# Eight gated blocks on one core: inverse square roots moved to VectorE, an MLP bias folded into a matmul, and three stages issued in written order

## The chip, the cores and the metric

The kernel runs on one core of a Trainium2 chip, in one launch. The metric is the device time of that launch in microseconds (us). A core has five engines that work side by side and meet only through semaphores: TensorE (PE; its weight loads are listed apart as PEld), VectorE (DVE), ScalarE (ACT), GpSimd (POOL) and SyncE (SP, which here only issues DMAs). Each engine takes its own instructions in the order in which they stand in its queue; an instruction whose semaphore is not there yet holds back all that stand behind it on that engine.

## The reference, cut to what matters

Four gated layers act on `x` of shape (16, 128, 128): 16 batches, 128 tokens, 128 features. Each layer adds a cross attention over a context of 77 rows and then a feed-forward block, each on a layer-normed `x` and scaled by the tanh of a gate:

```
x = x + tanh(g_xattn[i]) * Li_xattn(layernorm(x), ctx)
x = x + tanh(g_ffn[i])   * Li_ffn(layernorm(x))
```

The change touches three of the eight blocks. `L0_xattn` and `L2_xattn` are attentions with 16 heads of 8 features. `L0_ffn` is itself a stack of six transformer layers, and most of the time goes there:

```
for i in range(6):
    x = attn_layer(shift_tokens(x), ...) + x     # 16 heads of 64, q and k divided by their norms,
                                                 # rotary factors, window of 32, then Wo
    x = ffn_layer(shift_tokens(x), ...) + x      # layernorm, W1, a * gelu(gate), W2 + b2
```

`q` and `k` are divided by `max(norm, 1e-12)`; the second matmul of the MLP adds a bias `b2`.

## The kernel before

`X` lies in SBUF as four tiles of four batches each (groups `g` of 0 to 3, `GB` = 4). Everything is float32, apart from the attention mask. Blocks follow each other in the program: `l0_xattn`, `l0_ffn`, `l1_xattn` and so on. Within them a list scheduler of the Tile layer decides the order in which each engine's instructions stand: it takes what it thinks ready first, so that an engine's order is not that of the source.

**The heads of eight** (class `AttentionOf8`, called by `l0_xattn` and `l2_xattn`) go batch by batch in a software pipeline written in `run`: in round `n` the weights of batch n-2 are transposed (`turned`), the scores of batch n are made, masked and exponentiated (`scores`: PE, DVE L246 and L251, POOL L252, ACT L253), batch n-3 is mixed with its values (`mixed`), the weights of batch n-1 are divided by their sums (`normed`: DVE L257 and L258, POOL L259), and batch n-4 is projected and added to `X`. Scores have one PSUM buffer (tag `s`), all other PSUM tiles share four (tag `m`).

**The six layers** (`l0_ffn`) go by half units: a unit is one batch in one layer, and a half is 8 of its 16 heads. Step `k` of the loop takes five half units at different stages:

- half k ("a"): `l0_project` multiplies by Wqkv (PE L454), forms the rotary products out of PSUM (DVE L457, two of 128x1024), squares the same PSUM tile (ACT L462), sums the squares (DVE L463) and adds the rotary halves (POOL L466); `l0_values` makes the values (PE L471, ACT L473). After the second half of a unit, `l0_norms` turns the 32 sums of squares of each token into inverse roots: a maximum on POOL (L479), a first guess by an exponential of the bits (ACT L483), two Newton steps of four POOL instructions each (L485 to L488), and two POOL products that scale q and k (L492).
- half k-3 ("b"): `l0_turn` transposes q and k (PE, helper line L189) and copies them out; `l0_scores` makes masked scores (PE L505, L509), the row maximum (DVE L512), eight exponentials with their sums (ACT L516), and then the reciprocal (DVE L517) and the division (POOL L518).
- half k-5 ("c"): `l0_turn_p` transposes the weights (PE L189), `l0_mix` multiplies by the values (PE L532, copied by ACT L534).
- half k-7 ("d"): after the second half, `l0_add` multiplies by Wo (PE L540) and adds to `Y` (DVE L541).

A step with even `k` thus has `l0_add`; a step with odd `k` has `l0_norms`. At fixed steps, twice in each layer, two groups pass the MLP: `l0_mlp_norm` (token shift by a matmul, statistics on DVE L554 and L555, root on POOL L557 to L560, the bias b2 added to `Y` by POOL L561, normalised by ACT L563), two steps later `l0_mlp_turn` (transpose, gain and bias), and then `l0_mlp_out` for one group at a time (W1 on PE L576, gelu on ACT L578, product on DVE L579, W2 on PE L583, sum on DVE L584). PSUM is shared between two buffers of two banks for the big tiles (tag `s`: `ps_qk`, `ps_s`, `ps_h`) and four of one bank (tag `m`: all others).

Two engines that read the same PSUM tile are kept one after the other by the Tile layer, so the squares of L462 come after both products of L457.

Of the kernel before, what the change touches and what calls it, by code (L numbers as in the profile page):

```python
# [9 lines left out]
F32 = mybir.dt.float32  # L10
# [77 lines left out]
def tile_gated_layers(ctx: ExitStack, tc: tile.TileContext, io, out: bass.AP):  # L88
# [70 lines left out]

    def copy(i, out_, in_):  # L160

        if i % 2:
            nc.scalar.copy(out_, in_)  # L163
        else:
            nc.vector.tensor_copy(out_, in_)
# [7 lines left out]
    def layernorm(pool, out_, in_):  # L173

        st = pool.tile([128, GB, 6], F32, name="ln_st", tag="ln_st")
        mv = pool.tile([128, GB, 2], F32, name="ln_mv", tag="ln_mv")
        rs = pool.tile([128, GB], F32, name="ln_rs", tag="ln_rs")
        for j in range(GB):
            nc.vector.bn_stats(st[:, j, :], in_[:, j, :])
            nc.vector.bn_aggr(mv[:, j, :], st[:, j, :])  # L180
        rsqrt(pool, rs, mv[:, :, 1], GB, 1e-5)
        for j in range(GB):
            nc.vector.tensor_scalar(out_[:, j, :], in_[:, j, :], mv[:, j, 0:1], rs[:, j : j + 1], ALU.subtract, ALU.mult)

# [26 lines left out]
    class AttentionOf8:  # L211
# [28 lines left out]
        def scores(self, u, qT, kb):  # L240
            ps = self.psum.tile([128, 4, 512], F32, name="ps_s", tag="s")
            for c in range(4):
                at = slice(32 * c, 32 * c + 32)
                nc.tensor.matmul(ps[:, c, : 4 * S], lhsT=qT[at], rhs=kb[at], start=True, stop=True)
# [4 lines left out]
            )  # L249
            mx = self.pool.tile([128, 16], F32, name="mx", tag="mx")  # L250
# [10 lines left out]
        def turned(self, u):  # L261
            pT = u.pT = self.pool.tile([S, 16, 128], F32, name="pT", tag="pT")
            for c in range(4):
# [3 lines left out]
                nc.scalar.copy(pT[:, 4 * c : 4 * c + 4, :], pt[:S])  # L267

        def mixed(self, u, v):
            po = self.psum.tile([128, 4, 128], F32, name="ps_o", tag="m")  # L270
            for c in range(4):
                for t in range(4):
                    nc.tensor.matmul(po[32 * t : 32 * t + 32, c, :], lhsT=v[:, 4 * c + t, :], rhs=u.pT[:, 4 * c + t, :], start=True, stop=True)
            u.oT = self.pool.tile([128, 4, 128], F32, name="oT", tag="oT")
            nc.vector.tensor_copy(u.oT, po)

        def out(self, u):
# [3 lines left out]
            return pr  # L281

        def run(self, group, values, layer):

            class U:
                pass

            us = {}
            for n in range(-1, B + 4):
                if (n + 1) % GB == 0 and n + 1 < B:  # L290
                    ready = group((n + 1) // GB)
                    us.update({n + 1 + j: U() for j in range(GB)})
                    for j in range(GB):
                        us[n + 1 + j].qT, us[n + 1 + j].kb = ready[0][:, j, :], ready[1][:, :, j, :]
                if 0 <= n - 2 < B:
                    self.turned(us[n - 2])
                if 0 <= n < B:
                    self.scores(us[n], us[n].qT, us[n].kb)
                if 0 <= n - 3 < B:
                    self.mixed(us[n - 3], us[n - 3].v)  # L300
                if 0 <= n - 1 < B:
                    u = us[n - 1]
                    self.normed(u)
                    u.v = self.values(n - 1, values(n - 1))
                if 0 <= n - 4 < B:
                    pr = self.out(us[n - 4])
                    gated((n - 4) // GB, (n - 4) % GB, pr, tanh_x, layer)


    def l0_xattn():  # L310
        with tc.tile_pool(name="a0", bufs=2) as pool, tc.tile_pool(name="a0p", bufs=1, space=PSUM) as ps1, tc.tile_pool(
# [5 lines left out]
            def group(g):  # L317
# [5 lines left out]
                kb = attention.keys(kT)  # L323
                z = pool.tile([128, GB, 128], F32, name="z", tag="z")
                layernorm(pool, z, X[g])
                ps = transposed(psum, z)
                zT = pool.tile([128, GB, 128], F32, name="zT", tag="zT")
                nc.scalar.copy(zT, ps)
# [4 lines left out]
                return qT, kb  # L333
# [6 lines left out]
            attention.run(group, values, 0)  # L340


    def l0_ffn(weights):


        with tc.tile_pool(name="b0y", bufs=1) as ypool, tc.tile_pool(name="b0w", bufs=2) as wpool, tc.tile_pool(
# [12 lines left out]
            nc.vector.memset(seed, 0.5 * float(np.log(2.0)) * (127.0 - 0.043))  # L359
            W = {}  # L360
# [8 lines left out]
            for l in range(DEPTH):  # L369
                for part in range(2):  # L370
                    at = 2 * B * l + B * part + B + 7
                    pair = [_Mlp(l, 2 * part + i) for i in range(2)]
                    mlps.setdefault(at, []).extend((l0_mlp_norm, m) for m in pair)
                    mlps.setdefault(at + 2, []).extend((l0_mlp_turn, m) for m in pair)
                    mlps.setdefault(at + 3, []).append((l0_mlp_out, pair[0]))
                    mlps.setdefault(at + 5, []).append((l0_mlp_out, pair[1]))
# [9 lines left out]
            for k in range(2 * len(units) + B):  # L386
                a, ah = half_unit(k)
                b, bh = half_unit(k - 3)
                c, ch = half_unit(k - 5)
                d, dh = half_unit(k - 7)  # L390
                if a and ah == 0:
                    a.start(pool, W[a.l], xT[a.g][:, a.j, :])
                if b:
                    l0_turn(pool, psum, b, bh)
                if a:
                    l0_project(pool, psum, a, ah)
                if d and dh == 1:
                    l0_add(psum, d, Y[d.g][:, d.j, :])
                for part, m in mlps.get(k, ()):
                    part(pool, psum, W[m.l], Y[m.g], m)  # L400
                if c:
                    l0_turn_p(pool, psum, c, ch)
                if b:
                    l0_scores(pool, psum, b, bh, masks)
                if a:
                    l0_values(pool, psum, a, ah)
                if c:
                    l0_mix(pool, psum, c, ch)
                if a and ah == 1:
                    l0_norms(pool, a, seed)  # L410

                n, nh = half_unit(k + 2)
                if n and nh == 0 and n.j == 0:
                    shift(n)
# [3 lines left out]
    def l0_weights(wpool, l):  # L418
# [10 lines left out]
        w["b2"] = wpool.tile([128, 128], F32, name="w_b2", tag="w_b2")  # L429
        nc.sync.dma_start(out=w["b2"], in_=io["l0_b2"][l : l + 1].to_broadcast([128, 128]))  # L430
# [45 lines left out]
    def l0_norms(pool, u, seed):  # L476

        ss = u.ss.rearrange("p g a h -> p (g a h)")
        nc.gpsimd.tensor_scalar_max(ss, ss, 1e-24)  # L479
        y = pool.tile([128, 32], F32, name="nw_y", tag="nw_y")  # L480
        t = pool.tile([128, 32], F32, name="nw_t", tag="nw_t")

        nc.scalar.activation(y, ss.bitcast(I32), AF.Exp, bias=seed, scale=-0.5 * float(np.log(2.0)) / 2.0**23)  # L483
        for c in (1.0 + 1.67e-4, 1.0):
            nc.gpsimd.tensor_tensor(t, y, y, ALU.mult)  # L485
            nc.gpsimd.tensor_tensor(t, t, ss, ALU.mult)
            nc.gpsimd.tensor_scalar(t, t, -0.5 * c, 1.5 * c, ALU.mult, ALU.add)
            nc.gpsimd.tensor_tensor(y, y, t, ALU.mult)  # L488
        y = y.rearrange("p (g a) -> p g a", g=2)
        for g in range(2):  # L490
            r = u.r[g].rearrange("p a h d -> p (a h) d")
            nc.gpsimd.tensor_tensor(r, r, y[:, g].unsqueeze(2).to_broadcast([128, 16, 64]), ALU.mult)  # L492
# [7 lines left out]
    def l0_scores(pool, psum, u, g, masks):  # L500
# [16 lines left out]
        nc.vector.reciprocal(rs, rs)  # L517
        nc.gpsimd.tensor_tensor(p, p, rs.unsqueeze(2).to_broadcast([128, 8, 128]), ALU.mult)  # L518
        u.p.append(p)

# [22 lines left out]
    def l0_mlp_norm(pool, psum, w, Y, m):  # L543

        xs = m.xs = pool.tile([128, GB, 128], F32, name="xs", tag="xs")
# [536 lines left out]
```

## Time and profile before

| | |
|---|---|
| three timed runs | 3258.79, 3260.86 and 3262.26 us; median 3260.86 |
| the profiled execution's own time | 3258.67 us |
| its span in the profile | 3256.9 us, 50402 instructions |
| mean granted clock of TensorE | 0.915 of full speed |
| busy share of the span | PE 85%, PEld 58%, DVE 58%, ACT 54%, POOL 55% |
| `l0_xattn`, from the start | to 166 us |
| `l0_ffn` | 166 to 2205 us |
| `l2_xattn` | some 2555 to 2715 us |

The profile is one execution. Its views used here are: the table by stretch of time (busy time of each engine and the granted clock), the timeline (start, duration, engine, line, tiles; in brackets how long the engine had stood idle before and which instruction ended that), the list of waits, and the groups of instructions with the mean duration of one. A busy share is a mean over stages with different limits, so each stage has to be read by itself.

### The profile page before, as it was taken

Reading aid. Unit: us, or ns where it says so; the run is one execution under the profiler, and the core shown is the slowest. Engines: PE = TensorE matmul, PEld = TensorE weight load, DVE = VectorE, ACT = ScalarE, POOL = GpSimd, SP = SyncE. Lnnn points to the kernel's source line nnn. Section 1 sums busy time; section 2 is a strip of 40 time slices with the busy share of each in tenths; the row PEclk is TensorE's granted clock in tenths of the full one; section 3 lists DMA queues with packets and bytes.
Section 4 is the critical chain, followed back from the end, with each engine's and each line's share of the span. In section 5 each row is a group of like instructions: output and inputs, shape, how many; then the busy total and the mean of one; then the engine's idle time right before and its main releaser. Section 6 shows DMA issues by size and latency. Waiting matters only on the chain.

```text
span 3256.9 us, 50402 instructions
## 1 busy us (share of the span) xinstructions
PE 2756.5 (85%) x18912; PEld 1888.0 (58%) x18912; DVE 1876.6 (58%) x3163; ACT 1745.7 (54%) x5161; POOL 1778.9 (55%) x2030
## 2 busy tenths in 40 slices
PE   5779898989899898989898989898889678985656
PEld 4546565656566565656565656565655455653445
DVE  5566555555656564656565656545337765456553
ACT  3448676667667676758676767672222342222221
POOL 5568867686858585868776767751000451013222
PEclk8889999999999999999999999998779788997777
DMA  1020000000000000000000000002000000000003
GB/s 54 1 70 1 1 21 9 8 1 1 28 7 1 1 28 7 1 1 21 7 8 1 1 1 1 1 1 82 1 1 1 1 2 1 1 1 1 1 1 117
DMA packets 24304, 40.15 MB, mean 12 GB/s; under 512 B 1790, under 2 KB 18940, under 8 KB 22908
## 3 DMA queue, kind: packets, MB, share of 16 engines
q1 hardware_dynamic: 21036, 26.96, 2.5%
q0 software_dynamic: 2448, 9.07, 0.9%
q8 instruction: 149, 2.44, 0.3%
q10 hardware_dynamic: 576, 0.91, 0.1%
q14 instruction: 95, 0.78, 0.1%
HBM read 35.88 MB, written 1.05 MB: 11 GB/s over the span
## 4 chain that ended last, share of the span: by engine, by line
PE 46%; POOL 21%; ACT 15%; DVE 12%; issue 5%; DMA 1%; DVEq 0%; ACTq 0%; POOLq 0%
ACT p L516 7%; PE ps_t L189 7%; PE ps_qk L454 5%; POOL p L518 4%; POOL r L466 4%; PE ps_h L778 4%; POOL r L492 4%; PE ps_s L509 3%; PE ps_v L471 3%; DVE r L457 3%; PE ps_o L532 3%; PE ps_r L583 2%; PE ps_d L784 2%; PE ps_p L266 2%; PE ps_h L576 2%
## 5 line engine op out<-in xcount | busy, mean ns | idle before, releaser
L518 POOL TENSOR_TENSOR p<-p,rs 128x1024 f32<-128x1024 f32 x192 | 364.1, 1896 | 432.7 <-DVE rs L517 381.2
L516 ACT ACTIVATE p<-ps_s,mx 128x128 f32<-128x128 f32 x1536 | 539.6, 382 | 14.6 <-DVE mx L512 9.3
L457 DVE TENSOR_TENSOR r<-ps_qk,w_turn 128x1024 f32<-128x1024 f32 x384 | 454.2, 1215 | 140.2 <-PE ps_qk L454 74.8
L466 POOL TENSOR_TENSOR r<-r 128x512 f32<-128x512 f32 x384 | 480.7, 1271 | 9.5 <-DVE r L457 9.4
L454 PE MATMUL ps_qk<-w_qkv,xT 128*128 128x512 f32 x768 | 363.6, 596 | 5.3 <-ACT sq L462 3.3
L492 POOL TENSOR_TENSOR r<-r,nw_y 128x1024 f32<-128x1024 f32 x192 | 361.5, 1901 | 7.5
L516 ACT ACTIVATION_READ_ACCUMULATOR p<-ps_s,mx 128x1 f32 x1536 | 340.6, 222 | 0.0
L463 DVE TENSOR_REDUCE ss<-sq 128x16 f32<-128x1024 f32 x192 | 234.0, 1219 | 106.3 <-ACT sq L462 106.2
L189 PEld LDWEIGHTS ps_t<-const,p 128*128 128x128 f32 x1536 | 178.4, 143 | 168.8 <-ACT oT L534 110.3
L512 DVE TENSOR_REDUCE mx<-ps_s 128x8 f32<-128x1024 f32 x192 | 233.8, 1218 | 46.7 <-PE ps_s L509 46.7
L462 ACT ACTIVATE sq<-ps_qk 128x1024 f32<-128x1024 f32 x192 | 201.8, 1051 | 105.6 <-DVE r L457 103.2
L509 PEld LDWEIGHTS ps_s<-rT 64*128 64x128 f32 x3072 | 192.5, 193 | 104.1 <-ACT pT L163 49.0
L532 PEld LDWEIGHTS ps_o<-pT,v 128*64 128x64 f32 x3072 | 164.8, 137 | 122.4 <-issue 45.4
L509 PE MATMUL ps_s<-rT 64*128 64x128 f32 x3072 | 229.5, 290 | 5.8 <-ACT rT L163 5.8
L189 PE MATMUL ps_t<-const,r 128*128 128x128 f32 x1536 | 210.9, 281 | 17.2 <-POOL r L492 17.2
L471 PE MATMUL ps_v<-w_qkv,xT 128*128 128x512 f32 x384 | 224.6, 669 | 0.0
L505 PE MATMUL ps_s<-masks 128*128 128x512 bf16 x384 | 124.6, 392 | 116.8 <-ACT p L516 115.3
L473 ACT COPY v<-ps_v 128x512 f32<-128x512 f32 x192 | 114.3, 595 | 199.8 <-PE ps_v L471 199.8
L540 PEld LDWEIGHTS ps_r<-w_o,oT 128*128 128x128 f32 x1536 | 185.6, 192 | 59.5 <-issue 38.8
L189 PE MATMUL ps_t<-const,p 128*128 128x128 f32 x1536 | 212.3, 280 | 8.3 <-POOL nw_y L488 4.7
L532 PE MATMUL ps_o<-pT,v 128*64 128x128 f32 x3072 | 211.9, 279 | 1.8 <-ACT pT L163 1.2
L517 DVE RECIPROCAL rs<-rs 128x8 f32<-128x8 f32 x192 | 38.6, 201 | 300.5 <-ACT p L516 300.3
(265 smaller groups left out, 5275.9 us busy)
## 6 DMA issues: line engine op xcount, KB each, us to landing
w_qkv<-in_l_qkv SPq DMA_DIRECT2D x6, 1536.0 KB, 8.0
w_o<-in_l_o SPq DMA_DIRECT2D x6, 512.0 KB, 4.0
w<-in_l SPq DMA_DIRECT2D x6, 341.0 KB, 5.7
l_g<-in_l_g SPq DMA_DIRECT2D x1, 1152.0 KB
l_u<-in_l_u SPq DMA_DIRECT2D x1, 1152.0 KB, 11.1
l_d<-in_l_d SPq DMA_DIRECT2D x1, 1152.0 KB, 13.8
X<-in_x SPq DMA_DIRECT2D x4, 256.0 KB
l_kv<-in_l_kv SPq DMA_DIRECT2D x2, 512.0 KB, 14.4
```

What stands on the lines that cost most here:

```text
L189: nc.tensor.transpose(ps[:, j, :], in_[:, j, :], ident)
L454: nc.tensor.matmul(ps[:, a, :], lhsT=u.xT, rhs=u.w["qkv"][:, a * 1024 + g * 512 : a * 1024 + g * 512 + 512], start=True, stop=True)
L457: nc.vector.tensor_tensor(r12[:, :, a], ps[:, a].rearrange("p (h d) -> p h d", d=64).unsqueeze(1).to_broadcast([128, 2, 8, 64]), u.w["turn ...
L463: nc.vector.tensor_reduce(u.ss[:, g], sq.rearrange("p a (h d) -> p a h d", d=64), AX.X, ALU.add)
L466: nc.gpsimd.tensor_tensor(r[:, :, :, lo : lo + 32], r12[:, 0, :, :, lo : lo + 32], r12[:, 1, :, :, hi : hi + 32], ALU.add)
L471: nc.tensor.matmul(pv, lhsT=u.xT, rhs=u.w["qkv"][:, 2048 + g * 512 : 2048 + g * 512 + 512], start=True, stop=True)
L492: nc.gpsimd.tensor_tensor(r, r, y[:, g].unsqueeze(2).to_broadcast([128, 16, 64]), ALU.mult)
L509: nc.tensor.matmul(ps[:, o_, c, :], lhsT=u.rT[at, 0, c, :], rhs=u.rT[at, 1, c, :], start=False, stop=True, skip_group_check=True)
L512: nc.vector.tensor_reduce(mx, ps, AX.X, ALU.max, negate=True)
L516: nc.scalar.activation(p[:, h, :], ps[:, h, :], AF.Exp, bias=mx[:, h : h + 1], accum_out=rs[:, h : h + 1])
L518: nc.gpsimd.tensor_tensor(p, p, rs.unsqueeze(2).to_broadcast([128, 8, 128]), ALU.mult)
L532: nc.tensor.matmul(po[64 * o_ : 64 * o_ + 64, c, :], lhsT=u.v[g][:, 2 * c + o_, :], rhs=u.pT[:, 4 * o_ + c, :], start=True, stop=True)
```

## The change

1. **Order.** The loops of `AttentionOf8.run` and of `l0_ffn` are run inside `in_order`, which takes them out of the list scheduler's hands: PE, DVE, ACT and POOL issue these stages' instructions in the order in which the source emits them.
2. **Roots on VectorE.** In `l0_norms` the maximum before the root goes, the two Newton steps become six DVE instructions on a guess that now lies in PSUM (tag `m`), and a seventh DVE instruction bounds the result. The two scaling products stay on POOL.
3. **Division a step later.** The reciprocal and the division of `l0_scores` become `l0_divide`, called one step later, after `l0_project`.
4. **The bias b2.** It becomes an 86th row of the last part of W2; the matching row of the hidden tile is set to one once, and the POOL addition L561 goes. One DMA row of 128 floats replaces a DMA that spread the bias over 128 rows.
5. **The MLP in finer parts.** Statistics of both groups together at the end of step `at` (after `l0_norms`), normalisation at the end of step `at`+1, transposes at `at`+3, outputs at `at`+4 and `at`+6.
6. **Heads of eight in finer parts.** The layernorm is split into statistics (three rounds ahead), application on ACT (two rounds ahead, with the keys) and transposes (one round ahead); the transposes of the weights go in two halves around the scores; the copy of `oT` goes from DVE to ACT, and in `l2_xattn` the key bias too.

The diff, cut to its core:

```diff
+    def in_order(f, *args):
+        ET = mybir.EngineType
+        with tc.manual_schedule(engines={ET.PE, ET.DVE, ET.Activation, ET.Pool}):
+            f(*args)
...
+    def ln_stats(pool, in_):
...
+        for j in range(GB):
+            nc.vector.bn_stats(st[:, j, :], in_[:, j, :])
+        for j in range(GB):
+            nc.vector.bn_aggr(mv[:, j, :], st[:, j, :])
+        nc.gpsimd.tensor_scalar_add(rs[:, 0], mv[:, :, 1], 1e-5)
+        nc.gpsimd.tensor_tensor(rs[:, 0], rs[:, 0], minus_half[:, :GB], ALU.pow)
...
+    def ln_apply(out_, in_, rs):
+        for j in range(GB):
+            nc.scalar.activation(out_[:, j, :], in_[:, j, :], AF.Identity, bias=rs[:, 1, j : j + 1], scale=rs[:, 0, j : j + 1])
...
+            for n in range(-4, B + 4):
+                for k in (3, 2, 1):
...
+                if unit(n - 2):
+                    self.turned(us[n - 2], 0)
+                if unit(n):
+                    self.scores(us[n])
+                if unit(n - 2):
+                    self.turned(us[n - 2], 1)
+                if unit(n):
+                    self.exps(us[n])
+                if unit(n - 3):
+                    self.mixed(us[n - 3])
+                if unit(n - 1):
+                    self.normed(us[n - 1])
+                    us[n - 1].v = self.values(n - 1, values(n - 1))
+                if unit(n - 4):
+                    self.out(us[n - 4], n - 4, layer)
...
+            def steps():
+                for k in range(2 * len(units) + B):
...
+                    if b:
+                        l0_turn(pool, psum, b, bh)
+                    if a:
+                        l0_project(pool, psum, a, ah)
+                    if e:
+                        l0_divide(pool, e, eh)
+                    if d and dh == 1:
+                        l0_add(psum, d, Y[d.g][:, d.j, :])
+                    mlp_parts((k, 0))
+                    if c:
+                        l0_turn_p(pool, psum, c, ch)
+                    if b:
+                        l0_scores(pool, psum, b, bh, masks)
+                    if a:
+                        l0_values(pool, psum, a, ah)
+                    if c:
+                        l0_mix(pool, psum, c, ch)
+                    if a and ah == 1:
+                        l0_norms(pool, psum, a, seed)
+                    mlp_parts((k, 1))
...
+            in_order(steps)
...
-        w["b2"] = wpool.tile([128, 128], F32, name="w_b2", tag="w_b2")
-        nc.sync.dma_start(out=w["b2"], in_=io["l0_b2"][l : l + 1].to_broadcast([128, 128]))
+        nc.sync.dma_start(out=w["2"][85:86, 2, :], in_=io["l0_b2"][l : l + 1])
...
-        nc.gpsimd.tensor_scalar_max(ss, ss, 1e-24)
-        y = pool.tile([128, 32], F32, name="nw_y", tag="nw_y")
+        y = psum.tile([128, 32], F32, name="nw_y", tag="m")
...
         for c in (1.0 + 1.67e-4, 1.0):
-            nc.gpsimd.tensor_tensor(t, y, y, ALU.mult)
-            nc.gpsimd.tensor_tensor(t, t, ss, ALU.mult)
-            nc.gpsimd.tensor_scalar(t, t, -0.5 * c, 1.5 * c, ALU.mult, ALU.add)
-            nc.gpsimd.tensor_tensor(y, y, t, ALU.mult)
+            nc.vector.tensor_tensor(t, y, ss, ALU.mult)
+            nc.vector.scalar_tensor_tensor(t2, y, -0.5 * c, t, ALU.mult, ALU.mult)
+            nc.vector.scalar_tensor_tensor(y, t2, 1.5 * c, y, ALU.add, ALU.mult)
+        nc.vector.tensor_scalar_min(rn.rearrange("p g n -> p (g n)"), y, 1e12)
...
+    def l0_divide(pool, u, g):
+        nc.vector.reciprocal(u.rs, u.rs)
+        nc.gpsimd.tensor_tensor(u.p[g], u.p[g], u.rs.unsqueeze(2).to_broadcast([128, 8, 128]), ALU.mult)
...
+    def l0_mlp_stats(pool, psum, w, Y, ms):
...
+        for i, m in enumerate(ms):
...
+            nc.tensor.matmul(ps, lhsT=const_of("shift"), rhs=y[:, :, 64:128], start=True, stop=True)
+            nc.gpsimd.tensor_copy(xs[:, :, 0:64], y[:, :, 0:64])
+            nc.scalar.copy(xs[:, :, 64:128], ps)
+            for j in range(GB):
+                nc.vector.bn_stats(st[:, i, j, :], xs[:, j, :])
+                nc.vector.bn_aggr(mv[:, i, j, :], st[:, i, j, :])
...
-        nc.gpsimd.tensor_tensor(Y, Y, w["b2"].unsqueeze(1).to_broadcast([128, GB, 128]), ALU.add)
...
+                k = n + (c == 2)
+                nc.tensor.matmul(ps[:, j, :], lhsT=h[:k, c, j * 128 : (j + 1) * 128], rhs=w["2"][:k, c, :], start=c == 0, stop=c == 2)
```

Where the source now emits it, the order on an engine can be read off. DVE, in an odd step: copy of q (L165), two rotary products, sum of squares, reciprocal, row maximum, seven instructions of the root. DVE, in an even step: two rotary products, sum of squares, reciprocal, sum into `Y`, copy of the transposed weights, row maximum. ACT: copies of q and k, squares, copies of the transposed weights, eight exponentials, copy of the values, copy of `oT`, and in an odd step the first guess of the root. PE keeps the order that the list scheduler had found for a step: q and k transposes, Wqkv, Wo (even steps), transposes of the weights, masks, scores, values, mix. Lines in this document are those of the kernel before.

## The prediction

> **What bounds the kernel now.** I read the table by stretch of time first. The six layers are 2039 of the 3256.9 us and hold most of what the change touches; the two attentions of eight heads are 166 and 160 us.
>
> ```profile
> core 0: us, PE busy (x) PEld busy (x) DVE busy (x) ACT busy (x) POOL busy (x), PEclk, DMA share, GB/s
> 0.00:166.00 166.00, 110.02 (x1076) 82.58 (x1077) 97.23 (x148) 63.79 (x111) 86.65 (x48) 0.87 0.08 27
> 166.00:2205.00 2039.00, 1835.01 (x13325) 1235.68 (x13323) 1198.67 (x1600) 1414.05 (x4589) 1485.15 (x1806) 0.96 0.03 9
> 2555.00:2715.00 160.00, 112.89 (x1118) 86.79 (x1117) 101.57 (x160) 60.18 (x100) 82.07 (x39) 0.81 0.00 1
> ```
>
> In the six layers PE is busy 1835 of 2039 us at 0.96 of the clock: they are bound by PE, and only 204 us of PE's idle time can be won there. DVE has 840 us free, but free time on an engine is of use only in an order that lets it run ahead. So the timeline of one unit comes next (8 units with the same work make half a layer, 96 make the stage).
>
> ```profile
> 1505.99 1.23 DVE L512 TENSOR_REDUCE mx<-ps_s 128x8 f32<-128x1024 f32 x1
> 1506.09 1.02 ACT L462 ACTIVATE sq<-ps_qk 128x1024 f32<-128x1024 f32 x1 [0.93 <-DVE r L457]
> 1507.04 0.58 ACT L473 COPY v<-ps_v 128x512 f32<-128x512 f32 x1
> 1507.15 1.22 DVE L463 TENSOR_REDUCE ss<-sq 128x16 f32<-128x1024 f32 x1
> 1507.96 1.09 PE L189 MATMUL ps_t<-const,r 128*128 128x128 f32 x8
> ...
> 1510.73 0.39 ACT L483 ACTIVATE nw_y<-ss,seed 128x32 f32<-128x32 int32 x1
> 1510.86 2.36 DVE L457 TENSOR_TENSOR r<-ps_qk,w_turn 128x1024 f32<-128x1024 f32 x2
> 1513.33 1.02 ACT L462 ACTIVATE sq<-ps_qk 128x1024 f32<-128x1024 f32 x1 [1.25 <-DVE r L457]
> 1514.39 1.22 DVE L463 TENSOR_REDUCE ss<-sq 128x16 f32<-128x1024 f32 x1 [0.38 <-ACT sq L462]
> 1517.26 1.09 PE L189 MATMUL ps_t<-const,r 128*128 128x128 f32 x8 [0.23 <-POOL r L492]
> ```
>
> From 1500.74 to 1517.26 a unit takes 16.52 us. Three things matter. The squares follow the two rotary products (1510.86 + 2.36 = 1513.22, squares at 1513.33): the same PSUM tile. DVE fills that hole with the row maximum (1505.99) and sums the squares after it. And the roots on POOL let DVE start the next products (1510.86) while the first guess (1510.73) is still on ACT.
>
> Then the stalls of the MLP, of which there are 12:
>
> ```profile
> 377.98 1.90 POOL L492 TENSOR_TENSOR r<-r,nw_y 128x1024 f32<-128x1024 f32 x1
> ...
> 383.65 1.65 ACT L563 ACTIVATE xs<-xs,ln_rsm 128x128 f32<-128x128 f32 x4 [5.14 <-POOL ln_rsm L560]
> ...
> 386.73 0.58 PE L505 MATMUL ps_s<-masks 128*128 128x512 bf16 x1 [9.40 <-ACT p L516]
> ```
>
> ACT waits for a root on POOL behind two scalings, the exponentials stand behind that, and PE behind them: 9.4 us, with 1.5 us of smaller gaps. Half a layer takes 2039/12 = 169.9 us: 8 x 16.52 = 132.2, and 37.7 for the MLP with its stall.
>
> **The loop of a unit after the change.** In the written order DVE stands still in both places where it had been filled: it waits for the squares before it may do anything else, and in the odd step its seven root instructions wait for a guess that ACT issues behind eight exponentials and two copies. Nothing of the next step on DVE may pass them. I follow the closed circle, O for odd, E for even, gaps between engines (0.03 to 0.12 us, taken 0.09 or 0.04) as in the timeline:
>
> - Copy of the E weights done, PE mixes and starts step O: 0.09 + mix 1.02 + turns 0.93 + Wqkv 1.88 + 0.09 = 4.01.
> - O: products 2.36, 0.09, squares 1.02, 0.04, their sum 1.14, reciprocal 0.12, row maximum 1.22, 0.03 = 6.02.
> - ACT: eight exponentials 2.75, values 0.48, `oT` 0.46, guess 0.39, 0.04 = 4.12.
> - Roots on DVE, 0.03 more: no row has these shapes on DVE. Below, 7 x 0.18 = 1.3 (L851, 128x32); above, 7 x 0.34 + gaps = 2.6 (128x128, L194). Taken 1.78, nearer the row of the same width: 1.81.
> - E: products 2.36, 0.09, squares 1.02, 0.04, sum 1.14, reciprocal 0.12, sum into `Y` 0.20, weights copied 0.68 = 5.65.
>
> Sum 21.6 us against 16.52 (21.1 to 22.4 by the root's price). No engine is full in it: PE now waits some 5 us a unit.
>
> The transposes of E also need the PSUM buffer that the copy of the values frees, behind the exponentials: this makes one PE gap of some 3.2 us in each unit. What a gap does to the clock is read in `l2_xattn`, in the table by stretch and on PE's timeline:
>
> ```profile
> 2614.00:2619.00 5.00, 2.22 (x19) 1.61 (x16) 2.34 (x5) 1.49 (x2) 4.45 (x2) 1.00 0.00 0
> 2619.00:2623.00 4.00, 3.98 (x20) 3.34 (x20) 0.75 (x2) 2.33 (x4) 2.25 (x1) 0.57 0.02 4
> ```
> ```profile
> 2619.02 3.22 PE L266 MATMUL ps_p<-const,sm 128*77 128x128 f32 x16 [2.81 <-POOL sm L259]
> ```
>
> After 2.81 us of idle PE the granted clock goes from 1.00 to 0.57. In the loop 4.01 us are PE's. They cost nothing more if the clock holds, and some 2.3 more if the half clock lies over 60% of them. Taken about the middle, +1.0: 22.6 us a unit.
>
> The Trainium skill has a rule against this term ("TensorE: Matmul & The Clock Gate", section "HAM oscillation — how this bites in real kernels"): no harm from idle gaps up to about 3.4 us. By that rule the 3.2 us gap is free and the whole time some 96 us less; the row above, with 2.81 us, contradicts it.
>
> **The MLP, per half layer.** The old stall is gone: roots are asked for a step before they are used. New in its place, on the same circle:
> - Statistics at the end of an odd step: two copies on POOL stand behind both scalings (2 x 1.9 + 0.4), then eight pairs of statistics on DVE (0.27 + 0.17 by L554 and L555, 3.2 with gaps), all before DVE may go on: +7.4. PE idles about 8 us, and after the old stall's gap of 9.4 us the table shows 0.54 of the clock from 387 to 391 us; taken 5.7 us at half: +2.85. The eight normalisations on ACT (8 x 0.39 = 3.2) lie beside that; without that cover, +3.2.
> - Transposes: two products on DVE ahead of the weights' copy, +1.5.
> - Outputs, twice: the squares end, then a table load 1.28, gelu 0.7, product 0.75, the second W1 pair 2.0, gelu and product 1.45, W2 2.5, transposes 1.0, scores 1.5, row maximum 1.2, table load 1.3 with 0.4 of gaps = 14.1, where an ordinary step needs 2.5 to 3 from squares to exponentials: +11.3 each, 22.6.
> - Token shift of the next group: +1.
>
> Sum 35.4, about the 37.7 of now: the stall is paid back in outputs that nothing else fills. Half a layer is then 8 x 22.6 + 35.4 = 216.2, +46.3; twelve of them **+556 us**.
>
> **The attentions of eight heads.** A round now goes through its own chain: scores 0.8 to 1.4, mask 1.43, maximum 1.43, subtraction on POOL 2.25, sum of exponentials 1.43, product on POOL 2.25, then transposes 1.0 to 1.85. Both POOL steps fall in one round's turn, since `normed` of batch n-1 stands behind the subtraction of n and the next transposes wait for it: 9.2 to 10.7 us, taken 9.9 with gaps, against 8.3 a batch now (row maxima from 23.16 to 147.04 us). Sixteen batches and the shorter tail: **+19** in `l0_xattn` (+9 to +31), and **+10** in `l2_xattn` (0 to +20), which now has 8.4.
>
> **Costed at nothing.** The POOL addition L561 (2.5 us a pair) leaves an engine with 550 us free; were POOL the bound it would be -30 in all. The bias row: one DMA on SP of 128 floats for one that wrote 128 rows, in weights loaded a layer ahead, and one row more of a matmul's depth, which adds no column; behind them SP has only other weight loads. The memset is done once. The division a step later keeps POOL's work and moves it behind Wqkv; its user is a step away (POOL has 27% free in the stage). Were it late, its 1.9 us would fall on each of 192 half units, 365 us at most; here they lie beside the waits of the circle.
>
> **Rivals.**
> - A, the forecast: 3258.7 + 556 + 29 = **3844 us**, own range 3700 to 3960. Chance 0.50.
> - B, the clock holds and the statistics hide in part: 8 x 21.6 + 27 to 35 = 200 to 208 per half layer, so 3258.7 + 12 x (30 to 38) + 20 = 3640 to 3730. For it: the clock is 0.96 in a stage with many gaps under 2 us. Chance 0.22.
> - C, half clock in most units: 8 x 24 + 37 to 44 gives 229 to 236, 4000 to 4080. For it: the 2.81 us row. Chance 0.12.
> - D, the other side: the circle is broken (the guess is on ACT before DVE reaches the roots, or PE is far enough ahead that waits on DVE lie beside matmuls) and stays under PE's 16.52 us. Then PE keeps its rate and the twelve stalls go: 12 x 10.9 and some 2 us of half clock after each = 150, so about 3110. It decides below 16.5 us of circle; against it are 5 us. Chance 0.08, with it 0.01 for no change.
> - E, part of the circle is hidden, 17 to 19.5 us a unit: 3270 to 3560. Chance 0.07.
>
> **The numbers.** I name A, 3845 us, made against the profiled execution (3258.67 us, 1.8 over its span); the median of the runs shown is 2.2 higher, which is nothing here. The range leaves out D, most of E and the far end of C: 3560 to 4040. About 0.2% is what a measurement of this kernel can tell from no change: faster 0.08, within that 0.01, slower 0.91.
>
> **What would show it.** In the changed profile: a unit of some 22 us between first transposes; DVE idle ahead of the roots, put down to the guess on ACT, for about 4 us; DVE idle ahead of the sum of squares 1.1 us in nearly every half unit; a PE gap of 3 us ahead of the weights' transposes, released by the copy of the values; granted clock under 0.96 in the six layers; gelus with PE idle around them. If PE is above 95% busy between MLPs, the circle is wrong and D or E holds. If the unit is 21.6 and the clock 0.96, B.

## The result, and the profile after

Four runs of the kernel after gave 3934.68 to 3943.11 us, median **3936.71**, against 3260.82 before: 1.2076 times the time (95% interval 1.2058 to 1.2094). The forecast was 3845, with a range of 3560 to 4040. The profiled execution took 3943.11 us, its span is 3941.3. In the lines below L515 is Wqkv (L454 before), L518 the rotary products (L457), L523 and L524 the squares and their sum (L462, L463), L545 to L550 guess and roots, L553 the scalings (L492), L573 and L577 row maximum and exponentials (L512, L516), L534 and L598 the copies of values and `oT` (L473, L534), L214 the transposes (L189), L604 Wo (L540), L583 the division (L518).

The two traces, cut at the same events, show where the time lies:

| from, to | before | after | |
|---|---|---|---|
| start to the first Wqkv (`l0_xattn`) | 174.5 | 193.6 | +19.1 |
| first Wqkv to the last sum into `Y` (six layers) | 2058.1 | 2698.7 | +640.6 |
| to the first row maximum of `l2_xattn` | 327.4 | 329.1 | +1.7 |
| first to last row maximum of `l2_xattn` | 126.7 | 149.6 | +22.9 |
| to the end | 570.2 | 570.5 | +0.3 |

The table by stretch of time, kernel after, for the six layers:

```profile
core 0: us, PE busy (x) PEld busy (x) DVE busy (x) ACT busy (x) POOL busy (x), PEclk, DMA share, GB/s
187.00:2857.00 2670.00, 2101.80 (x13273) 1371.03 (x13274) 1316.01 (x2262) 1417.05 (x4586) 1245.49 (x876) 0.89 0.02 7
```

PE was busy 1835 of 2039 us; now it is 2102 of 2670: it waits for 568 us, and the clock (0.89 against 0.96) has made the same matmuls 267 us longer. VectorE has 117 us more to do and GpSimd 240 us less, but neither is near its limit. The groups of instructions say what the engines wait for (last columns: idle time just ahead of the group, and what ended it). Two of the kernel before, then four of the kernel after:

```profile
L454 PE MATMUL ps_qk<-w_qkv,xT 128*128 128x512 f32 x768 | 363.6, 596 | 5.3 <-ACT sq L462 3.3
L463 DVE TENSOR_REDUCE ss<-sq 128x16 f32<-128x1024 f32 x192 | 234.0, 1219 | 106.3 <-ACT sq L462 106.2
```
```profile
L515 PE MATMUL ps_qk<-w_qkv,xT 128*128 128x512 f32 x768 | 496.5, 783 | 5.0 <-ACT sq L523 3.3
L214 PE MATMUL ps_t<-const,r 128*128 128x128 f32 x1536 | 270.2, 315 | 293.3 <-ACT v L534 270.0
L524 DVE TENSOR_REDUCE ss<-sq 128x16 f32<-128x1024 f32 x192 | 234.2, 1220 | 225.8 <-ACT sq L523 225.8
L547 DVE TENSOR_TENSOR nw_t<-nw_y,ss 128x32 f32<-128x32 f32 x192 | 36.8, 191 | 429.4 <-ACT nw_y L545 426.1
```

VectorE stands 1.2 us ahead of each of 192 sums of squares and 4.4 us ahead of each of 96 roots; PE stands 270 us in all ahead of the transposes of q and k (the forecast's list of signs had named those of the weights), for the copy of the values; a matmul of Wqkv takes 783 ns where it took 596. One ordinary unit (timeline, even step; weight loads and all but the last exponential left out):

```profile
1932.95 0.40 ACT L577 ACTIVATE p<-ps_s,mx 128x128 f32<-128x128 f32 x1
...
1933.29 0.63 ACT L534 COPY v<-ps_v 128x512 f32<-128x512 f32 x1
1933.76 0.65 ACT L598 COPY oT<-ps_o 128x512 f32<-128x512 f32 x1
...
1933.97 0.66 PE L214 MATMUL ps_t<-const,r 128*128 128x128 f32 x4 [3.29 <-ACT v L534]
...
1934.24 0.36 ACT L545 ACTIVATE nw_y<-ss,seed 128x32 f32<-128x32 int32 x1
...
1934.46 2.94 PE L515 MATMUL ps_qk<-w_qkv,xT 128*128 128x512 f32 x4
...
1934.63 0.19 DVE L547 TENSOR_TENSOR nw_t<-nw_y,ss 128x32 f32<-128x32 f32 x1 [4.19 <-ACT nw_y L545]
...
1935.99 0.19 DVE L550 TENSOR_SCALAR rn<-nw_y 128x32 f32<-128x32 f32 x1
...
1937.51 2.35 DVE L518 TENSOR_TENSOR r<-ps_qk,w_turn 128x1024 f32<-128x1024 f32 x2 [1.33 <-PE ps_qk L515]
...
1939.96 1.02 ACT L523 ACTIVATE sq<-ps_qk 128x1024 f32<-128x1024 f32 x1 [4.37 <-DVE r L518]
...
1941.02 1.22 DVE L524 TENSOR_REDUCE ss<-sq 128x16 f32<-128x1024 f32 x1 [1.15 <-ACT sq L523]
```

The wait for the guess is there as forecast, 4.19 us. But the roots are through at 1936.18, and the products start at 1937.51: they wait for Wqkv, which took 2.94 us in place of 1.88, behind transposes that had waited 3.29 us for the buffer of the values. From guess to guess the units of half a layer take 23.8, 23.8, 25.2, 31.6, 38.8, 35.1, 24.1 and 22.8 us, 225.2 in all (170.0 before). Below, the first, second and last unit of a half layer are called ordinary; over the ten half layers from the second to the eleventh they take 23.3 us in the mean (16.5 before), and a half layer takes 223.1.

**Theories.** "Roots" is the forecast's: row maximum, exponentials, guess and roots on VectorE hold the next products. "Slot" is what the trace of after suggests: exponentials, copy of the values, PSUM buffer, transposes, Wqkv at half clock. The rival to both is that the roots matter in any order, or that no place in it matters and the written order costs as such.

### The profile page after: what moved, and what is told of

Same layout as the page of the kernel before. It is cut to its first block, busy times and chain, and to the rows that moved or that the text cites. A ratio compares the mean times of both kernels' runs of the same rounds, so it can differ in the third digit from the quotient of the medians.

```text
span 3941.3 us, 50238 instructions
## 1 busy us (share of the span) xinstructions
PE 3046.9 (77%) x18912; PEld 2036.4 (52%) x18912; DVE 1959.3 (50%) x3759; ACT 1780.9 (45%) x5229; POOL 1542.5 (39%) x1119
## 3 DMA queue, kind: packets, MB, share of 16 engines
HBM read 35.49 MB, written 1.05 MB: 9 GB/s over the span
## 4 chain that ended last, share of the span: by engine, by line
PE 47%; DVE 24%; ACT 18%; POOL 6%; issue 3%; DMA 0%; ACTq 0%; DVEq 0%; POOLq 0%
PE ps_qk L515 10%; ACT p L577 9%; PE ps_t L214 7%; DVE r L518 7%; DVE ss L524 4%; ACT sq L523 4%; DVE mx L573 3%; PE ps_h L846 3%; PE ps_s L570 3%; PE ps_r L604 3%; PE ps_o L596 2%; PE ps_d L852 2%; POOL sm L287 2%; PE ps_v L532 2%; PE ps_r L654 2%
## 5 line engine op out<-in xcount | busy, mean ns | idle before, releaser
L577 ACT ACTIVATE p<-ps_s,mx 128x128 f32<-128x128 f32 x1536 | 540.8, 378 | 396.6 <-DVE mx L573 390.0
L553 POOL TENSOR_TENSOR r<-r,rn 128x1024 f32<-128x1024 f32 x192 | 361.2, 1903 | 717.5 <-DVE rn L550 712.6
L518 DVE TENSOR_TENSOR r<-ps_qk,w_turn 128x1024 f32<-128x1024 f32 x384 | 451.8, 1218 | 330.1 <-PE ps_qk L515 326.3
L515 PE MATMUL ps_qk<-w_qkv,xT 128*128 128x512 f32 x768 | 496.5, 783 | 5.0 <-ACT sq L523 3.3
L214 PE MATMUL ps_t<-const,r 128*128 128x128 f32 x1536 | 270.2, 315 | 293.3 <-ACT v L534 270.0
L523 ACT ACTIVATE sq<-ps_qk 128x1024 f32<-128x1024 f32 x192 | 196.9, 1026 | 629.2 <-DVE r L518 519.9
L583 POOL TENSOR_TENSOR p<-p,rs 128x1024 f32<-128x1024 f32 x192 | 364.4, 1898 | 21.6 <-DVE rs L582 17.0
L214 PEld LDWEIGHTS ps_t<-const,r 128*128 128x128 f32 x1536 | 190.6, 158 | 352.4 <-ACT v L534 289.6
L524 DVE TENSOR_REDUCE ss<-sq 128x16 f32<-128x1024 f32 x192 | 234.2, 1220 | 225.8 <-ACT sq L523 225.8
L577 ACT ACTIVATION_READ_ACCUMULATOR p<-ps_s,mx 128x1 f32 x1536 | 334.2, 218 | 0.0
L596 PEld LDWEIGHTS ps_o<-pT,v 128*64 128x64 f32 x3072 | 189.2, 143 | 269.8 <-issue 163.4
L596 PE MATMUL ps_o<-pT,v 128*64 128x128 f32 x3072 | 252.4, 290 | 97.3 <-DVE pT L171 67.2
L604 PEld LDWEIGHTS ps_r<-w_o,oT 128*128 128x128 f32 x1536 | 237.6, 235 | 83.2 <-issue 80.1
L573 DVE TENSOR_REDUCE mx<-ps_s 128x8 f32<-128x1024 f32 x192 | 230.4, 1200 | 55.3 <-PE ps_s L570 55.3
L547 DVE TENSOR_TENSOR nw_t<-nw_y,ss 128x32 f32<-128x32 f32 x192 | 36.8, 191 | 429.4 <-ACT nw_y L545 426.1
L515 PEld LDWEIGHTS ps_qk<-w_qkv,xT 128*128 128x128 f32 x768 | 173.8, 250 | 143.4 <-issue 137.1
L214 PE MATMUL ps_t<-const,p 128*128 128x128 f32 x1536 | 211.4, 276 | 34.0 <-DVE Y L605 23.7
L604 PE MATMUL ps_r<-w_o,oT 128*128 128x128 f32 x1536 | 228.9, 313 | 0.0
```

The lines of the kernel that those rows point to most:

```text
L214: nc.tensor.transpose(ps[:, j, :], in_[:, j, :], ident)
L515: nc.tensor.matmul(ps[:, a, :], lhsT=u.xT, rhs=u.w["qkv"][:, a * 1024 + g * 512 : a * 1024 + g * 512 + 512], start=True, stop=True)
L518: nc.vector.tensor_tensor(r12[:, :, a], ps[:, a].rearrange("p (h d) -> p h d", d=64).unsqueeze(1).to_broadcast([128, 2, 8, 64]), u.w["turn ...
L523: nc.scalar.activation(sq, ps, AF.Square)
L524: nc.vector.tensor_reduce(u.ss[:, g], sq.rearrange("p a (h d) -> p a h d", d=64), AX.X, ALU.add)
L553: nc.gpsimd.tensor_tensor(r, r, rn[:, g].unsqueeze(2).to_broadcast([128, 16, 64]), ALU.mult)
```

## The experiments

Times are single executions beside 3261 us for the kernel before, unless an interval is given; the four of the kernel after lie within 8.4 us.

**e1_free: no written order.**
```diff
-        with tc.manual_schedule(engines={ET.PE, ET.DVE, ET.Activation, ET.Pool}):
-            f(*args)
+        f(*args)
```


> Everything of the change but the written order: the list scheduler orders all stages again. Theory 'roots' (as predicted: the roots on VectorE hold the next products until the guess comes from behind eight exponentials): the scheduler also puts the seven root instructions ahead of the next products, so the wait stays, about 2.75 + 0.46 + 0.39 + 0.04 + 1.55 = 5.2 us between row maximum and next products; the copy of the values now stands ahead of the exponentials, so the loop is near 21 us and the time 3550 to 3750. Theory 'order' (what costs is the written order alone; roots on VectorE are free): PE keeps its 16.5 us, the stalls of the MLP shrink, 3110 to 3260.

Measured: **3270.83**, 1.003 times before (1.002 to 1.004). Neither range held it: the theory "roots" had expected the scheduler to keep the wait in every unit, and in ordinary units it does not. It issues the next products first and the roots behind them. All else of the change together is worth +10 us; the written order is worth +666. The unit is 18.1 us, not 16.5, and the timeline tells why:

```profile
1191.72 0.19 DVE L547 SCALAR_TENSOR_TENSOR nw_y<-nw_t,nw_y 128x32 f32<-128x32 f32 x1
...
1192.01 1.90 POOL L581 TENSOR_TENSOR p<-p,rs 128x1024 f32<-128x1024 f32 x1
...
1193.87 3.77 POOL L551 TENSOR_TENSOR r<-r,rn 128x1024 f32<-128x1024 f32 x2
...
1195.83 1.09 PE L212 MATMUL ps_t<-const,r 128*128 128x128 f32 x8 [1.05 <-POOL r L551]
```

The scalings stand behind the division (L581) on GpSimd and come 1.05 us late for the transposes. What this loses the shorter MLP gives back (units of 22.1, 24.6, 26.8 and 24.1 us in place of 28.7, 27.8, 26.8 and 18.9).

**e2_double: four Newton steps.** `for c in (1.0 + 1.67e-4, 1.0, 1.0, 1.0)`.


> Four Newton steps in place of two (six more VectorE instructions of 0.19 us, 1.35 us a unit with gaps). Theory 'roots': they are on the circle, +1.35 x 96 = +130, some 4065. Theory 'slot' (from the trace of after: the next products wait for Wqkv, which waits for the transposes of the even step, which wait for the PSUM buffer that the copy of the values frees behind the exponentials; at half clock Wqkv ends 1.3 to 2.0 us after the roots): the added steps fill that slack, 0 to +20, 3937 to 3960.

3965.95, +29, just over the range of "slot" and far under that of "roots": in the order of after the roots are not on the loop, but for the little that exceeds their slack. For "slot", against "roots".

**e3_vfirst: values copied ahead of the exponentials.** The eight exponentials move out of `l0_scores` into a function called after `l0_values`.
```diff
                         l0_values(pool, psum, a, ah)
+                    if b:
+                        l0_exps(pool, b, bh)
```


> Written order, but ScalarE copies the values ahead of the eight exponentials. Theory 'slot': the transposes and Wqkv of the even step no longer wait for the exponentials; the next products wait for the roots instead, 1.3 to 2.0 us earlier, -130 to -190, 3745 to 3810. Theory 'roots': these were on the circle all along, only what the clock lost comes back, 0 to -100, 3840 to 3937.

3764.89, -172: "slot". The ordinary unit is 20.8 us in 21 of 32 cases (21.1 to 22.8 in the others), and now the products follow the roots at once:

```profile
1520.08 0.19 DVE L561 TENSOR_SCALAR rn<-nw_y 128x32 f32<-128x32 f32 x1
1520.19 2.34 DVE L520 TENSOR_TENSOR r<-ps_qk,w_turn 128x1024 f32<-128x1024 f32 x2
```

**e12_vf_double: the same with four Newton steps.**


> As e3_vfirst (values copied ahead of the exponentials), with four Newton steps in place of two: 1.35 us more of VectorE work a unit. In the order of after the same addition cost 29 us (e2_double). If with the values first the loop goes through the guess and the roots, it costs all of it: +100 to +130 over e3_vfirst, 3865 to 3895. If the roots are not on the loop there either: up to +40, 3765 to 3805.

3963.44, +199, above both ranges: once the buffer is out of the way the loop does go through the roots. The addition cost 3.0 us a unit (20.8 to 23.8), 1.35 by itself; the rest, in the unit below, is the clock. On PE's timeline, e3_vfirst and then e12_vf_double:

```profile
1243.10 1.09 PE L602 MATMUL ps_o<-pT,v 128*64 128x128 f32 x16 [1.86 <-DVE pT L171]
1244.13 1.09 PE L214 MATMUL ps_t<-const,r 128*128 128x128 f32 x8
1245.06 1.88 PE L517 MATMUL ps_qk<-w_qkv,xT 128*128 128x512 f32 x4
```
```profile
1326.32 1.09 PE L602 MATMUL ps_o<-pT,v 128*64 128x128 f32 x16 [3.22 <-DVE pT L171]
1327.35 1.97 PE L214 MATMUL ps_t<-const,r 128*128 128x128 f32 x8
1329.11 2.73 PE L517 MATMUL ps_qk<-w_qkv,xT 128*128 128x512 f32 x4
```

The gap ahead of the mix grew from 1.86 to 3.22 us, and the transposes and Wqkv behind it then took 1.73 us more.

**e8_ysbuf: guess in SBUF.**
```diff
-        y = psum.tile([128, 32], F32, name="nw_y", tag="m")
+        y = pool.tile([128, 32], F32, name="nw_y", tag="nw_y")
```


> Only the first guess moves from PSUM to SBUF, so that the four PSUM buffers rotate by 13 and not by 14 tiles a unit; the copy of the values keeps its place behind the exponentials. Theory 'slot' (the transposes of the even step wait for the buffer of the values): they now get the buffer of a copy made earlier, the gap of 3.3 us goes or moves, 3745 to 3830, as with the values first. If it is the place of the copy on ScalarE that counts and not the buffer: 3920 to 3950.

3871.76, -65, between the two ranges: the direction of "slot", with half of its size. The transposes of the even step no longer wait, and the products follow the roots (the last root starts at 1063.60, the products at 1063.69). But Wo waits for the values in their place (1.13 us), and a gap of 2.4 us ahead of the mix keeps half clock in the odd step. That one PSUM tile of 128 bytes a row turned the rotation of four buffers is shown; the copy early (e3_vfirst) is worth more.

**e4_warm: PE kept busy.** In odd steps the mix is issued three times more into the same tile.


> In every odd step the matmuls that mix weights and values run three times more into the same PSUM tile, before it is copied: same result, PE is busy for 3 us in the gap ahead of the next transposes. If the half clock after the gap is on the circle: Wqkv of the even step takes 1.88 in place of 2.9 to 3.3 us and the products wait for the roots, 1.2 us earlier a unit, -80 to -180, 3755 to 3855. If the clock costs nothing on the circle: 3937 or up to 30 more.

3808.08, -129. All Wqkv of ordinary units run at 1.88 us, no PE gap of over 0.9 us is left between matmuls there, and the unit is 21.6 us: **the half clock costs 1.7 us a unit in the mean** (23.3 to 21.6), and 2.2 in those of 23.8. At full clock the transposes still follow the copy of the values, but the roots and Wqkv end nearly together (the last root at 1279.04):

```profile
1276.83 0.66 PE L214 MATMUL ps_t<-const,r 128*128 128x128 f32 x4 [0.67 <-ACT v L534]
1277.32 1.88 PE L515 MATMUL ps_qk<-w_qkv,xT 128*128 128x512 f32 x4
1278.85 0.19 DVE L550 TENSOR_SCALAR rn<-nw_y 128x32 f32<-128x32 f32 x1
1279.31 2.36 DVE L518 TENSOR_TENSOR r<-ps_qk,w_turn 128x1024 f32<-128x1024 f32 x2 [0.27 <-PE ps_qk L515]
```

The kernel after holds its own check: ahead of three of its ordinary units (from 391.0, 612.9 and 834.4 us) PE's gap was the same 3.29 us as elsewhere, but the clock stayed at 1.00 behind it, and these units took 21.6 us. So most of what e3_vfirst won is the clock too: with the clock held, the early copy takes the unit from 21.6 to 20.8.

**e6_poolroots: roots back on GpSimd, order kept.** `l0_norms` as before.


> Written order, with the roots back on GpSimd as in the kernel before (their maximum and eight small steps, guess in SBUF); all else as after. Theory 'order with roots' (the order costs because VectorE waits in it for the guess): the next products no longer wait, some 18.2 us a unit, half a layer near 181 us, 3400 to 3560. Theory 'order alone' (the place of the roots does not matter in the written order): 3850 to 3950.

3622.32, -314, in neither range: the place of the roots matters a great deal in this order, but the gain was sized 60 to 220 us too large. The unit is 18.9 to 20.3 us. The division now stands behind roots and scalings on GpSimd, and the transposes of the weights wait for it: their weight loads 136 us in 61 places in the list of waits, about 2.2 us each.

**e5_vf_late: values first, and the roots a step later, behind the products.** `l0_norms` ends with the guess; the seven instructions become `l0_roots`.
```diff
+        if late is not None:
+            l0_roots(late)          # behind the rotary products, ahead of the squares
```


> Written order with the values copied ahead of the exponentials, the first guess in SBUF, and the seven root instructions moved one step later, behind the next rotary products (one scaling ahead of the division on GpSimd, one behind). Theory 'slot, then roots': with the copy early the unit was 20.8 us, bound by exponentials, guess and roots ahead of the products; now the products start after the row maximum and the loop goes through the squares of the even step, which ScalarE issues behind the exponentials: some 18.0 us, 2.8 less, 3470 to 3590. Theory 'PE or buffers' (something else holds the even step now): no more than 40 below the run with the values first, 3725 to 3765.

3701.18, only 64 below e3_vfirst: missed. Units of 20.3 us and more. The seven root instructions take 3.4 us here, as in the next run, where the cause is seen best; what makes some units 22 to 23 us was not tried.

**e9_repaired: row maximum ahead of the sum of squares (odd), copy of the weights ahead of it (even).**


> As e5_vf_late, and VectorE also takes the row maximum ahead of the sum of squares in odd steps, and the copy of the weights ahead of it in even steps, as the scheduler's order had it: nothing on VectorE stands idle behind the squares. Theory 'order of VectorE': the loop falls below PE's work, 16.5 to 17 us a unit; with 35 us for the MLP half a layer takes 167 to 172 us, 3270 to 3350. If a written order as such costs (the MLP, or PE's order): over 3400.

3568.18, unit 19.0: the range of "order of VectorE" is missed, and the rival's (over 3400, the written order as such) holds it. But the timeline, behind the products, names another cause for a part of it:

```profile
904.11 0.19 DVE L591 SCALAR_TENSOR_TENSOR nw_t<-nw_y,nw_t 128x32 f32<-128x32 f32 x1
904.12 2.54 POOL L557 TENSOR_TENSOR r<-r 128x512 f32<-128x512 f32 x2 [18.06 <-DVE nw_t L590]
...
904.34 1.15 DVE L592 SCALAR_TENSOR_TENSOR nw_y<-nw_t,nw_y 128x32 f32<-128x32 f32 x1
...
905.53 1.19 DVE L590 TENSOR_TENSOR nw_t<-nw_y,ss 128x32 f32<-128x32 f32 x1
...
907.52 1.90 POOL L598 TENSOR_TENSOR r<-r,rn 128x1024 f32<-128x1024 f32 x1 [0.86 <-DVE rs L461]
```

Two of the seven root instructions take 1.15 and 1.19 us instead of 0.19: each ends as one of the two GpSimd sums beside it ends. The seven take 3.5 us in place of 1.6 (from the start of the first, 903.90, to the end of the last, 907.38). The scaling behind the two sums then waits 0.86 us more for VectorE, so it is the roots that hold it, and not the sums.

**e10_port: the first scaling ahead of these GpSimd sums.** One edit of order, so that GpSimd has nothing to do while VectorE makes the roots.
```diff
-                    if a:
-                        l0_rsums(pool, a)
                     if late:
                         l0_scale(late, 0)
+                    if a:
+                        l0_rsums(pool, a)
```


> As e9_repaired, with one edit on GpSimd: in even steps the first scaling stands ahead of the two sums of the rotary halves, so that GpSimd is idle while VectorE does the seven root instructions. In e9_repaired two or more of these took 1.15 to 1.19 us instead of 0.19, each as long as a GpSimd instruction beside it was still running (guess in SBUF). Theory 'VectorE is held while GpSimd works, when both its inputs are in SBUF': the roots fall from 3.5 to 1.6 us, some 1.5 to 1.9 us a unit, 3390 to 3450. If the long instructions have another cause: 3540 to 3600.

3400.79, -167. The groups of e9_repaired and then of e10_port (mean ns of one behind the comma):

```profile
L590 DVE TENSOR_TENSOR nw_t<-nw_y,ss 128x32 f32<-128x32 f32 x192 | 126.7, 660 | 6.0 <-ACT nw_y L584 2.8
L592 DVE SCALAR_TENSOR_TENSOR nw_y<-nw_t,nw_y 128x32 f32<-128x32 f32 x192 | 118.2, 615 | 6.5
```
```profile
L592 DVE SCALAR_TENSOR_TENSOR nw_y<-nw_t,nw_y 128x32 f32<-128x32 f32 x192 | 36.8, 192 | 6.5
L590 DVE TENSOR_TENSOR nw_t<-nw_y,ss 128x32 f32<-128x32 f32 x192 | 35.8, 186 | 6.1 <-ACT nw_y L584 2.8
```

The same instructions, 660 and 615 ns beside GpSimd, 186 and 192 without. The unit is 17.8 us. What is left over e1_free, 3401 against 3271, is what the rival can claim: the written order as such. A written order can thus come up to the scheduler's in ordinary units; the four round the MLP (25.2, 33.6, 30.9 and 16.8 us) still take 106.5 us together, against 97.6 in e1_free.

**e7_xs: after, with GpSimd's copies for the statistics ahead of the scalings.**


> Kernel after, with GpSimd's two copies for the statistics of the MLP ahead of the roots and the two scalings, twelve times. Theory of the forecast (VectorE waits for those copies, 4.2 us in the trace of after, and all of the next step with it): -4 us and up to 3 us of half clock, twelve times, -45 to -85, 3850 to 3892. If the statistics lie beside PE's work: 3920 to 3940.

3878.15, -59, or 4.9 us for each of the twelve: the statistics are on the path, as forecast.

**e11_poolorder: the version that the runs point to.** The scheduler orders all engines but GpSimd, which issues the six layers in written order, one scaling ahead of the division; guess in PSUM; copies for the statistics early; heads of eight left to the scheduler. These edits were tried together only.
```diff
-        with tc.manual_schedule(engines={ET.PE, ET.DVE, ET.Activation, ET.Pool}):
+        with tc.manual_schedule(engines={ET.Pool}):
```


> The version that the runs point to: the list scheduler orders PE, VectorE and ScalarE everywhere; only GpSimd issues the six layers in written order, one scaling ahead of the division (in e1_free the transposes of the odd step wait 1.05 us for the scalings behind it), copies for the statistics early, guess in PSUM, roots written one step later. Theory 'scaling too late in e1_free': the unit goes from 18.1 to 16.5 to 17.1 us, -100 us or a little less, 3140 to 3220. If the roots on VectorE cost PE time in any order: 3255 to 3290.

**3178.85**, 0.9754 times before (0.9737 to 0.9770). The unit is 17.0 us; the scaling starts right after the last root, and the transposes no longer wait for it:

```profile
1007.09 0.18 DVE L598 TENSOR_SCALAR rn<-nw_y 128x32 f32<-128x32 f32 x1
...
1007.42 1.91 POOL L603 TENSOR_TENSOR r<-r,rn 128x1024 f32<-128x1024 f32 x1 [0.28 <-DVE rn L598]
...
1009.28 1.90 POOL L627 TENSOR_TENSOR p<-p,rs 128x1024 f32<-128x1024 f32 x1
...
1009.79 1.09 PE L214 MATMUL ps_t<-const,r 128*128 128x128 f32 x8
```

In this version the roots run beside GpSimd too (369 of 672 beside its 128x512 sums), and each takes 183 to 192 ns in the mean: their guess lies in PSUM.

## Why the prediction was right, and where it was wrong

- **Direction, place and size.** 3845 forecast, 3937 measured; six layers +556 against +640. That the written order, not any engine's work, sets the unit is shown: the order taken off gives 3271, the roots moved in it 3622, the order repaired 3401.
- **The loop of 21.6 us.** Its sum is right where the loop exists as drawn: in e3_vfirst, the forecast's circle less the copy of the values (0.48) and with the roots as measured (1.57 with gaps, 1.78 taken), it is 20.9 against a measured 20.8. In the kernel after it is not the circle that closes in most units. The step that failed is "the guess and the roots ahead of the next products": they are done 1.3 us before the products can start. In their place stand the PSUM buffer of the values, four transposes and Wqkv at half clock (e2_double +29, e3_vfirst -172). The forecast had seen the buffer, but only as a cause of half clock. With a full clock both ways end nearly together: in e4_warm the last root ends at 1279.04 and the products start at 1279.31, so the same 21.6 us came out. That the forecast's sum fits there is in part luck: the other way, which it did not add up, happens to be 0.3 us longer.
- **The clock, +1.0 a unit.** Mis-sized: 1.7 in the mean (e4_warm, 23.3 to 21.6), 2.2 in units of 23.8, where the clock was 0.50 behind the gap. The missing 0.7 on 96 units is 67 us of the 92 that the forecast was short; the rest is some 14 in the MLP and 13 in `l2_xattn`. It was taken at the middle of 0 to 2.3; the row of 2.81 us, which spoke for the upper end, was the better guide for most units.
- **The Trainium skill's rule** weighed there ("TensorE: Matmul & The Clock Gate", section "HAM oscillation — how this bites in real kernels": no harm from gaps up to about 3.4 us) does not hold here: gaps of 3.2 to 3.3 us cost 1.7 us a unit in the mean.
- **The MLP, +35.4.** Measured 36.6 in the mean of ten half layers (223.1 less eight ordinary units). Of its terms, the unit of the statistics is 8.0 over an ordinary one (10.25 forecast), the two of the outputs 14.9 and 11.3 (22.6 in all forecast, 26.2 measured), turn and shift 2.3 (2.5). That the sum fits is thus partly two errors that cancel. Only the statistics were tested by themselves (e7_xs); the others are read from the trace.
- **Heads of eight.** A round was put at 9.9 us; it takes 9.89 in `l0_xattn` and 9.97 in `l2_xattn`. `l0_xattn` came out at +19.1 (+19 forecast). `l2_xattn` at +23: the forecast's +10 did not follow from its own round, 15 x (9.9 - 8.45) = 22.
- **Costed at nothing.** The division a step later and the bias row are both in e1_free, which is only 10 us longer than before; they were not tried alone. The division is not free there: it stands ahead of the scalings on GpSimd, which come 1.05 us late in each unit, and the shorter MLP makes up for it.
- **The rival on the other side** (3110: PE keeps its rate and the stalls go) was not far off as a possibility of the parts: e11_poolorder has PE busy 93% of the stage and takes 3179. It fails for the change as made, because the order stands in the way.

What stays open: why the four units round the MLP take 9 us more in e10_port than in e1_free; and `l0_xattn`, which takes 8 to 10 us more than before even under the scheduler (first Wqkv at 182.1 and 184.7 in e1_free and e11_poolorder, 174.5 before).

## What to carry to other kernels

Fix by hand the order of one engine whose queue the scheduler gets wrong, not of all: a written order turns every wait for another engine into a wait of all that stands behind it, and VectorE here had three in each unit, for two sets of squares and a guess. Before work is moved to an engine that has time free, follow the circle of the loop through it, and through the buffers that its tiles rotate among, since a small tile in a shared pool can change who waits for whom. When a forecast wait makes a gap on PE, price the matmuls behind it at the clock that the nearest gap in the trace was followed by.

## What the runs showed of the hardware

**Gaps and the clock.** For each gap of PE in the six layers I took the mean granted clock of the 2 us behind it. Under 0.85 it was after 1 of 122 gaps of 0.9 to 1.6 us (e10_port; the one ahead of the first Wqkv), 18% of 104 of 1.6 to 2.2 us (e3_vfirst), 54% of 70 of 2.2 to 2.8 us (e8_ysbuf), and 94% and 96% of 70 and 82 of 2.8 to 3.4 us (after, e12_vf_double). By kernel the share for the same length differs widely (1.6 to 2.2 us: 0% of 22 in e10_port, 58% of 26 in after; 2.2 to 2.8 us: 36% of 80 in e5_vf_late; 2.8 to 3.4 us: 64% of 25 in e9_repaired, 14% of 14 in e6_poolroots), so the length of a gap alone does not decide, and what else does is open. There is no sharp limit in these runs, and the harm begins below 2 us: in e3_vfirst it followed 17 of 103 gaps of 1.6 to 2.0 us, with the clock at 1.00 before them.

**VectorE beside GpSimd.** A root instruction on 128x32 took 0.19 us alone and up to 1.27 us while GpSimd added 128x512 tiles, when all its inputs were in SBUF (e9_repaired; over 0.3 us in 190 of 672, just two in each of 95 units); moved away from GpSimd's work it took 0.19 (e10_port), and with the guess in PSUM 0.18 to 0.20 beside the same work (e11_poolorder; e1_free likewise). No run moves the guess alone beside such work. The Trainium skill ("SBUF — State Buffer", section "SBUF: two separate sides") tells of a port pair that VectorE with two SBUF inputs and GpSimd lock from each other for a whole instruction; the runs agree, with about 1.0 us as the price here.
